# Layer 0's attention scores: from four-pass products of 48 rows to three one-pass products of exact 12-bit halves, 64 rows per head

## The chip, the cores and the metric

The kernel runs on one core of a Trainium2 chip. The metric is the device time of a whole execution in microseconds, from three runs; a profile is taken of a further execution. In the profile's names PE is TensorE (PEld its weight loads), DVE is VectorE, ACT is ScalarE, POOL is GpSimd, and SPq is the queue of DMA issues on SyncE.

## What is computed

Input x is 8 images of 384 channels and 32 x 32 pixels (1024 tokens), in fp32. Two layers follow. Layer 0 is attention over a group-normalized image, with a relative bias; layer 1 is a second attention (6 heads of 64, normalized q and k) and a feed-forward with binarized weights. The change is in layer 0:

```python
tokens = x.reshape(b, c, n).transpose(0, 2, 1)
qkv = (tokens @ qkv_w + qkv_b).reshape(b, n, 3, NUM_HEADS, HEAD_DIM)
...
q, k, v = (qkv[0], qkv[1], qkv[2])
scale = HEAD_DIM ** (-0.5)
attn = jnp.einsum('bhnd,bhmd->bhnm', q * scale, k)
attn = attn + _relative_bias(h, w, mlp_w1, mlp_b1, mlp_w2, mlp_b2)[None]
attn = jax.nn.softmax(attn, axis=-1)
out = jnp.einsum('bhnm,bhmd->bhnd', attn, v)
```

There are 8 heads of 48 dimensions; each head and image needs a score matrix of 1024 x 1024.

## The kernel before, in words

Layer 0 (`_layer0`) works image by image. For each image it projects q and k (`project_qk`, L464), then v (`project_v`, L498), and then runs 32 units. A unit (pair, h, m2) is one pair of heads (j = 0 and 1), one half h of the 1024 queries and 256 of the 1024 keys.

- `project_qk` makes, for three tiles of 128 rows and for q and k, a product of six fp32 matmul calls, three blocks of input channels times two halves of 512 tokens (L475); each call is two records in the profile. VectorE evicts q with bias and scale (L485), ScalarE evicts k with its bias (L489). A tile holds two heads of 48 rows in the lower parts of its two 64-row halves; the 16 rows left over in each half carry a third of the heads of pair 3, which six DMAs an image (L492) gather into pair 3's tile.
- `scores` (L522) issues for a unit eight fp32 matmuls (L529): 48 rows (the head's dimensions) by 64 keys, over 512 queries. j picks the upper or lower 64 rows of the array, c the left or right 64 columns, so that four of them have a quarter of the array each. Then it calls `weigh` for the unit two before, and after that VectorE adds the bias out of the table `grow` while it reads PSUM (L540), and ScalarE takes the exponential (L544).
- `weigh` (L549) multiplies a unit's exponentials with v, eight fp32 matmuls of 64 x 64 (L560), into one accumulator for a pair and half; after four units ScalarE and VectorE evict it (L568, L571), and after both halves `divide` (L574) writes the row sums to memory, reads them spread out (L588), has GpSimd take the reciprocal (L589), writes it (L590) and, some steps later, reads it back over 64 rows (L597) for a multiplication on GpSimd (L601).
- `project_out` for the image before comes at unit 3: 36 records of L624, three VectorE adds with the residual (L640), which was loaded by L634, and three writes of 512 KB (x<-res, L643).
- PSUM has four buffers of two banks (`mm2`). The accumulator holds one of them, a unit's two score tiles hold two. Exponentials, residuals and the pieces of the bias table share nine buffers of 512 KB (`etile`).

The order on each engine is the order of the calls: the pools and semaphores only add waits. Work that is spread over the units is hung on `_Later`, whose `step()` is called after each block of a projection and after each unit. In image 0 the relative bias is built this way: a table of 8 x 3969 values is written to memory (L387), and 32 pieces (head h, quarter c) are read from it, each by four DMAs on the SP queue (`grow_load`, L399, first into `etile` buffers named wide, later into oT) and turned by a copy (`grow_turn`, L409 on ScalarE for even c, L411 on VectorE for odd c). All these DMAs, and those of q and k, the residuals and the reciprocals, go through the one SP queue in order. A DMA there also waits until the eighth before it has landed.

The feed-forward of layer 1 already uses one-pass matmuls: L1578 and L1629 take operands of type F32R, an fp32 that was split into a rounded part and a remainder, and are one record for each call, with 128 x 128 weights.

Of the kernel before, what the change touches and what calls it, by code (L numbers as in the profile page):

```python
# [27 lines left out]
P = 128  # L28
QP = P // 2
# [12 lines left out]
FR = D0 // NF0  # L42
HID = 192
# [144 lines left out]
def _layer0(tc, ins, x1, sums, shared, weights, beside):  # L188
# [9 lines left out]
    with ExitStack() as ctx:  # L198
        const = ctx.enter_context(tc.tile_pool(name="a_const", bufs=1))
        qkp = ctx.enter_context(tc.tile_pool(name="a_qk", bufs=NP0))  # L200
        ep = ctx.enter_context(tc.tile_pool(name="a_e", bufs=9))
# [5 lines left out]
        def etile(name, shape=(P, N)):  # L207
            return ep.tile(list(shape), F32, tag="e", name=name)
# [44 lines left out]
        def load(b):  # L253
# [15 lines left out]
        assert FR == S0 - D0  # L269
        both = shared.weights("w0")  # L270
        wqk = both[:, 0 : KC * 2 * C].rearrange(
            "p (k s h d) -> p k s h d", k=KC, s=2, d=S0
        )
        wv = both[:, KC * 2 * C :].rearrange("p (k c) -> p k c", k=KC)
        bqk = const.tile([P, 2, NF0], F32, tag="bqk", name="bqk")
# [21 lines left out]
        def place_weights_qk():  # L297
            whole = 2 * NF0 * D0
            for s in range(2):
                nc.vector.tensor_copy(  # L300
                    wqk[:, :, s, :, 0:D0],
                    raw[:, :, s, 0:whole].rearrange("p k (h d) -> p k h d", d=D0),
                )
                for j in range(2):
                    at = whole + j * D0
                    nc.vector.tensor_copy(
                        wqk[:, :, s, j::2, D0:S0],
                        raw[:, :, s, at : at + D0].rearrange("p k (c d) -> p k c d", d=FR),
                    )

        def load_bias_qk():
            with nc.allow_non_contiguous_dma(reason="a bias, once"):
                for j in range(2):
                    for row, n, at, step in (
                        (j * S0, D0, j * D0, 2 * D0),
                        (j * S0 + D0, FR, (2 * NF0 + j) * D0, FR),
                    ):
                        for s in range(2):
                            nc.sync.dma_start(
                                bqk[row : row + n, s],  # L320
                                bass.AP(
                                    qkv_b.tensor, qkv_b.offset + s * C + at, [[1, n], [step, NF0]]
                                ),
                            )
# [139 lines left out]
        def project_qk(b, xn):  # L464

            qk = {
                pair: qkp.tile([P, 2, N], F32, tag="qk", name=f"qk{b}_{pair}") for pair in range(NP0)
            }
            for pair in range(NF0):
                t = qk[pair]  # L470
                for s in range(2):
                    pq = mm2(f"pq{b}_{pair}_{s}")
                    for k in range(KC):
                        for h in range(NH):
                            nc.tensor.matmul(  # L475
                                pq[:, h],
                                wqk[:, k, s, 2 * pair : 2 * pair + 2, :].rearrange(
                                    "p h d -> p (h d)"
                                ),
                                xn[:, k, ts(h, HALF)],  # L480
                                start=(k == 0), stop=(k == KC - 1),
                            )
                    bias = bqk[:, s, pair : pair + 1]
                    if s == 0:
                        nc.vector.tensor_scalar(  # L485
                            t[:, s], flat2(pq), bias, D0**-0.5, ALU.add, ALU.mult
                        )
                    else:
                        nc.scalar.activation(t[:, s], flat2(pq), AF.Identity, bias=bias)  # L489
                    later.step()  # L490
                for j in range(2):
                    nc.sync.dma_start(  # L492
                        qk[NF0][j * S0 + pair * FR : j * S0 + (pair + 1) * FR],
                        t[j * S0 + D0 : (j + 1) * S0],
                    )
            return qk
# [25 lines left out]
        def scores(b, qk, u, weigh):  # L522
            pair, h, m2 = u
            s = [mm2(f"s{b}_{pair}_{h}_{m2}_{j}") for j in range(2)]
            for i in range(2):
                for c in range(2):
                    for j in range(2):
                        rows = slice(j * S0, j * S0 + D0)
                        nc.tensor.matmul(  # L529
                            s[j][ts(c, QP), i], qk[pair][rows, 1, ts(4 * m2 + 2 * i + c, QP)],  # L530
                            qk[pair][rows, 0, ts(h, HALF)], start=True, stop=True,
                        )
# [155 lines left out]
        qk = project_qk(0, first)  # L688
        project_v(0, first)
        for b in range(B):  # L690
            held = []
            for i, u in enumerate(units):
# [8 lines left out]
                if i == 3 and b > 0:  # L701
                    project_out(b - 1, residuals(b - 1, etile), range(NF0))
                if b == B - 1:
                    for at, work in beside:
                        if at == i:
                            work()
                later.step()
            if b + 1 < B:
                qk = project_qk(b + 1, xn)
# [1197 lines left out]
```

## Time and profile before

| what | value |
|---|---|
| median of 3 runs | 3038.4 us (3035.8 to 3039.46) |
| span of the profiled execution, first to last instruction | 3031.8 us |
| median less that span | 6.6 us |
| mean granted TensorE clock | 0.999 |
| records on TensorE, busy | 18902, 3010.9 us |
| DMA traffic | 153.47 MB, mean 51 GB/s |
| layer 0's scores, L529 | 4096 records, 607.8 us busy |
| layer 0's weighing, L560 | 4096 records, 603.8 us busy |

The profile gives no time of its execution but the span, so sums are made against the span. "Busy" of a group is the time in which at least one of its instructions ran; since matmuls overlap, a group's mean duration is far longer than the distance from one start to the next. The timeline merges neighbours of one group into a line: start, time from the first start to the last end, and how many.

### The profile page before, as it was taken

What the parts mean: (1) busy time and instruction counts of PE and PEld (TensorE: products, weight loads), DVE (VectorE), ACT (ScalarE), POOL (GpSimd) and SP (SyncE); (2) the same over time, 40 slices, a digit from 0 to 9 for tenths busy, and PEclk for the clock granted to TensorE, in tenths of its full rate; (3) what the DMA queues carried; (4) which work ended last, traced back from release to release, by engine and by line L of the source; (5) the groups of instructions that cost most, each with busy time, mean ns of one, the idle gap of its engine ahead of it and who ended that gap; (6) DMA issues with size and microseconds to landing.
All of it is one profiled execution on the core that took longest, in us unless ns stands there. A gap on an engine that the chain in (4) does not pass through costs nothing.

```text
span 3031.8 us, 45645 instructions
## 1 busy us (share of the span) xinstructions
PE 3010.9 (99%) x18902; PEld 1622.9 (54%) x18902; DVE 1777.3 (59%) x1765; ACT 1401.8 (46%) x1757; POOL 470.2 (16%) x314
## 2 busy tenths in 40 slices
PE   8999999999999999999999999999999999999999
PEld 3555546455554645555545655655655655645453
DVE  3746637374654727364565765765765755755646
ACT  2633526253452615254463553553653543653534
POOL 2111102121110202102202202202202202211110
PEclk9999999999999999999999999999999999999999
DMA  7512020210202021121401101101101101102011
GB/s 199 146 26 83 19 83 17 72 37 19 83 19 83 23 72 30 26 99 51 116 27 37 50 16 37 50 23 30 50 23 30 50 23 30 50 16 72 16 51 38
DMA packets 102425, 153.47 MB, mean 51 GB/s; under 512 B 59648, under 2 KB 63216, under 8 KB 101184
## 3 DMA queue, kind: packets, MB, share of 16 engines
q1 hardware_dynamic: 98944, 148.63, 17.0%
q8 instruction: 152, 2.49, 0.3%
q10 hardware_dynamic: 3264, 1.82, 0.2%
q14 instruction: 65, 0.53, 0.1%
HBM read 112.29 MB, written 29.07 MB: 47 GB/s over the span
## 4 chain that ended last, share of the span: by engine, by line
PE 93%; DVE 2%; DMA 2%; SPq 1%; ACT 1%; POOL 0%; issue 0%; DVEq 0%; ACTq 0%; POOLq 0%
PE s L529 15%; PE o L560 15%; PE s L1337 11%; PE o L1386 11%; PE pq L475 8%; PE y2p L1629 6%; PE pq L1193 5%; PE pp L624 4%; PE pv L1274 4%; PE y1p L1578 4%; PE pp L1483 4%; PE pv L503 4%; SPq L399 1%; PE sum L1413 1%; PE hs L1222 1%; DVE lun L1530 1%
## 5 line engine op out<-in xcount | busy, mean ns | idle before, releaser
L544 ACT ACTIVATE e<-e 128x1024 f32<-128x1024 f32 x512 | 535.0, 1057 | 441.1 <-DVE e L540 419.9
L540 DVE TENSOR_TENSOR e<-s,grow 128x1024 f32<-128x1024 f32 x512 | 601.1, 1218 | 186.3 <-PE s L529 186.3
L529 PE MATMUL s<-qk 48*64 48x512 f32 x4096 | 607.8, 591 | 2.8 <-DVE e L540 2.7
L560 PE MATMUL o<-e,v 64*64 64x512 f32 x4096 | 603.8, 589 | 0.0
L1348 ACT ACTIVATE e<-s,kc 128x512 f32<-128x512 f32 x768 | 463.9, 694 | 170.6 <-PE s L1337 160.0
L1337 PE MATMUL s<-qk,qk 64*64 64x512 f32 x3072 | 418.3, 592 | 0.2
L1386 PE MATMUL o<-e,v 64*64 64x512 f32 x3072 | 414.8, 590 | 0.0
L529 PEld LDWEIGHTS s<-qk 48*64 48x64 f32 x4096 | 242.2, 132 | 222.1 <-issue 74.9
L560 PEld LDWEIGHTS o<-e,v 64*64 64x64 f32 x4096 | 266.7, 133 | 171.0 <-issue 63.0
L1363 DVE TENSOR_TENSOR t<-t,e 128x1024 f32<-128x1024 f32 x192 | 230.9, 1221 | 53.9 <-ACT e L1348 53.9
L1337 PEld LDWEIGHTS s<-qk,qk 64*64 64x64 f32 x3072 | 153.5, 132 | 189.9 <-issue 110.3
L1193 PE MATMUL pq<-bx,wqkv 128*128 128x512 f32 x576 | 254.1, 596 | 0.7 <-ACT tra L1165 0.7
L475 PE MATMUL pq<-xn,w 128*128 128x512 f32 x576 | 251.8, 598 | 0.0
L1386 PEld LDWEIGHTS o<-e,v 64*64 64x64 f32 x3072 | 157.6, 133 | 171.1 <-issue 143.8
L589 POOL TENSOR_TENSOR inv<-sums,over 128x16 f32<-128x16 f32 x32 | 92.8, 2900 | 956.9 <-DMA sums<-sd 785.4
L475 PEld LDWEIGHTS pq<-xn,w 128*128 128x128 f32 x576 | 109.4, 191 | 142.4 <-issue 139.9
L1193 PEld LDWEIGHTS pq<-bx,wqkv 128*128 128x128 f32 x576 | 107.8, 190 | 143.5 <-issue 139.7
L1360 DVE TENSOR_TENSOR t<-e,e 128x1024 f32<-128x1024 f32 x96 | 114.1, 1224 | 83.0 <-ACT e L1348 83.0
L1565 DVE TENSOR_REDUCE parts<-y 128x1 f32<-128x1024 f32 x75 | 90.1, 1217 | 93.7 <-ACT y L1562 93.2
L1243 POOL TENSOR_TENSOR hc<-hc,rsqrt 128x32 f32<-128x32 f32 x24 | 139.0, 5793 | 2.0
L1209 ACT ACTIVATE qsq<-pq 128x1024 f32<-128x1024 f32 x48 | 49.2, 1025 | 190.1 <-DVE qk L1203 101.9
L485 DVE TENSOR_SCALAR qk<-pq,bqk 128x1024 f32<-128x1024 f32 x24 | 30.8, 1283 | 178.3 <-PE pq L475 178.3
(166 smaller groups left out, 3034.3 us busy)
## 6 DMA issues: line engine op xcount, KB each, us to landing
rb<-rd SPq DMA_DIRECT2D x110, 256.0 KB
xn<-in_x_dram SPq DMA_DIRECT2D x24, 512.0 KB
res<-in_x_dram SPq DMA_DIRECT2D x24, 512.0 KB
x<-res SPq DMA_DIRECT2D x24, 512.0 KB
bx<-x SPq DMA_DIRECT2D x8, 1536.0 KB
rq<-hi SPq DMA_DIRECT2D x48, 256.0 KB
out_dram<-bx SPq DMA_DIRECT2D x23, 512.0 KB
wide<-table SPq DMA_DIRECT2D x80, 114.2 KB
```

The lines of the kernel that those rows point to most:

```text
L475: nc.tensor.matmul(pq[:, h], wqk[:, k, s, 2 * pair : 2 * pair + 2, :].rearrange("p h d -> p (h d)"), xn[:, k, ts(h, HALF)], start=(k == 0) ...
L529: nc.tensor.matmul(s[j][ts(c, QP), i], qk[pair][rows, 1, ts(4 * m2 + 2 * i + c, QP)], qk[pair][rows, 0, ts(h, HALF)], start=True, stop=True,)
L540: nc.vector.tensor_add(e.rearrange("p (i q) -> p i q", i=2), s[j], bass.AP(near.tensor, near.offset, [near.ap[0], [-QROWS * IW, 2], [1, HA ...
L544: nc.scalar.activation(e, e, AF.Exp)
L560: nc.tensor.matmul(po[ts(j, S0), r], v[keys, 2 * m2 + i, 2 * pair + j, :], es[j][keys, ts(i, HALF)], start=(m2 == 0 and i == 0), stop=(m2 ...
L1193: nc.tensor.matmul(pq[:, h], wqkv[:, k, s * C + pair * P : s * C + (pair + 1) * P], xt[:, k, ts(h, HALF)], start=(k == 0), stop=(k == KC - 1),
L1243: nc.gpsimd.tensor_tensor(c, c, rsqrt.to_broadcast(list(c.shape)), ALU.pow)
L1337: nc.tensor.matmul(s[j][ts(c, QP), i], qk[pair, 1][rows, ts(4 * m2 + 2 * i + c, QP)], qk[pair, 0][rows, ts(h, HALF)], start=True, stop=True,)
L1348: nc.scalar.activation(e[:, ts(i, HALF)], s[j][:, i], AF.Exp, scale=kc[:, pair, j, m : m + 1])
L1363: nc.vector.tensor_add(total[j], total[j], e)
L1386: nc.tensor.matmul(po[ts(j, D1), r], v[keys, 2 * m2 + i, at : at + D1], es[j][keys, ts(i, HALF)], start=(m2 == 0 and i == 0), stop=(m2 == ...
L1629: nc.tensor.matmul(py[m][:, h], w2[:, k, ts(m, P)], supply.parts[k][i][:, ts(h, HALF)], start=(k == 0 and i == 0), stop=(k == FC - 1 and i ...
```

## The change

q and k are split, on eviction, into a rounded part (high) and what is left (low), both of type F32R, so that a product of parts needs one pass of TensorE. q . k is then the sum of four products of parts. To fill 64 rows of the array, the head's 48 dimensions are cut into 32 (DA) and 16 (DB):

- The first 32 dimensions of a head give 64 rows of alternating high and low. `q1` and `k1` in the same order give high.high + low.low; `k1x`, with the two swapped, gives the cross products.
- The last 16 dimensions give 32 rows, twice: `q2` holds them twice, `k2` once in order and once swapped, so one product gives all four.

So a head's scores are three accumulated products of 64 rows, and each matmul takes 128 keys at once: 12 matmul calls a unit of one record each, instead of 8 of two. The two heads of a pair still have the upper and the lower 64 rows.

The columns of the weights are put in the order that this needs (two blocks of 128 with the first 32 dimensions of four heads each, one block with the last 16 of all eight), and q's scale goes into weights and bias. The six evictions of an image each become one on ScalarE (high) and one on VectorE (low). Both parts are written to memory (12 writes of 512 KB an image), and the tiles q1, k1, k1x, q2 and k2 of a pair are read back in their layout by nine DMAs (2.5 MB a pair), `load_pair`: for pair 0 inside the projection, for pair p + 1 in the second unit of pair p. All of them are issued on the SP queue; the six DMAs of L492 go. The projection's `etile` buffers hold the parts until they are written, and there are eight of them instead of nine.

```diff
@@ -40,6 +40,9 @@
+DA = 32
+DB = D0 - DA
+NB0 = C // P
...
-        qkp = ctx.enter_context(tc.tile_pool(name="a_qk", bufs=NP0))
-        ep = ctx.enter_context(tc.tile_pool(name="a_e", bufs=9))
+        qkp = ctx.enter_context(tc.tile_pool(name="a_qk", bufs=2))
+        ep = ctx.enter_context(tc.tile_pool(name="a_e", bufs=8))
...
-        def etile(name, shape=(P, N)):
-            return ep.tile(list(shape), F32, tag="e", name=name)
+        def etile(name, shape=(P, N), dtype=F32):
+            return ep.tile(list(shape), dtype, tag="e", name=name)
...
         def place_weights_qk():
-            whole = 2 * NF0 * D0
             for s in range(2):
-                nc.vector.tensor_copy(
-                    wqk[:, :, s, :, 0:D0],
-                    raw[:, :, s, 0:whole].rearrange("p k (h d) -> p k h d", d=D0),
-                )
-                for j in range(2):
-                    at = whole + j * D0
-                    nc.vector.tensor_copy(
-                        wqk[:, :, s, j::2, D0:S0],
-                        raw[:, :, s, at : at + D0].rearrange("p k (c d) -> p k c d", d=FR),
-                    )
+                given = raw[:, :, s].rearrange("p k (h d) -> p k h d", d=D0)
+                for at, n, d0, d in ((0, H0 * DA, 0, DA), (H0 * DA, H0 * DB, DA, DB)):
+                    to = wqk[:, :, s, at : at + n].rearrange("p k (h d) -> p k h d", d=d)
+                    of = given[:, :, :, d0 : d0 + d]
+                    if s == 0:
+                        nc.vector.tensor_scalar_mul(to, of, D0**-0.5)
+                    else:
+                        nc.vector.tensor_copy(to, of)
...
+            nc.gpsimd.tensor_scalar(bqk[:, 0], bqk[:, 0], D0**-0.5, 1.0, ALU.mult, ALU.mult)
...
         def project_qk(b, xn):
-            qk = {
-                pair: qkp.tile([P, 2, N], F32, tag="qk", name=f"qk{b}_{pair}") for pair in range(NP0)
-            }
-            for pair in range(NF0):
-                t = qk[pair]
-                for s in range(2):
-                    pq = mm2(f"pq{b}_{pair}_{s}")
-                    for k in range(KC):
-                        for h in range(NH):
-                            nc.tensor.matmul(
-                                pq[:, h],
-                                wqk[:, k, s, 2 * pair : 2 * pair + 2, :].rearrange(
-                                    "p h d -> p (h d)"
+            halves, qk = {}, {}
+            blocks = [(blk, s) for blk in (NB0 - 1, *range(NB0 - 1)) for s in range(2)]
+            for n, (blk, s) in enumerate(blocks):
+                pq = mm2(f"pq{b}_{blk}_{s}")
+                for k in range(KC):
+                    for h in range(NH):
+                        nc.tensor.matmul(
+                            pq[:, h], wqk[:, k, s, ts(blk, P)], xn[:, k, ts(h, HALF)],
+                            start=(k == 0), stop=(k == KC - 1),
+                        )
+                bias = bqk[:, s, blk : blk + 1]
+                high = etile(f"hq{b}_{blk}_{s}", dtype=F32R)
+                low = etile(f"lq{b}_{blk}_{s}", dtype=F32R)
+                nc.scalar.activation(high, flat2(pq), AF.Identity, bias=bias)
+                nc.vector.scalar_tensor_tensor(
+                    low, flat2(pq), bias, high.bitcast(F32), ALU.add, ALU.subtract
+                )
+                there = dram.tile([P, 2, N], F32, tag=f"hl{blk}{s}", name=f"hl{b}_{blk}_{s}")
+                for x, part in enumerate((high, low)):
+                    nc.sync.dma_start(there[:, x], part.bitcast(F32))
+                halves[blk, s] = there
+                if n in (2, 3, 4):
+                    load_pair(b, 0, halves, qk, n - 2)
+                later.step()
+            return halves, qk
+        def load_pair(b, pair, halves, qk, part):
+            blk, row = pair // 2, pair % 2 * S0
+            if part == 0:
+                at = 2 * pair * DB
+                for name, s in (("q2", 0), ("k2", 1)):
+                    t = qkp.tile([P, N], F32R, tag=name, name=f"{name}_{b}_{pair}")
+                    src = halves[NB0 - 1, s]
+                    qk[pair, name] = t
+                    for j in range(2):
+                        first = src.offset + (at + j * DB) * 2 * N
+                        if s == 0:
+                            nc.sync.dma_start(
+                                t[ts(j, S0)].bitcast(F32),
+                                bass.AP(src.tensor, first, [[0, 2], [N, 2 * DB], [1, N]]),
+                            )
+                            continue
+                        for y in range(2):
+                            nc.sync.dma_start(
+                                t[j * S0 + y * DA : j * S0 + (y + 1) * DA].bitcast(F32),
+                                bass.AP(
+                                    src.tensor, first + y * N,
+                                    [[2 * N, DB], [N - 2 * y * N, 2], [1, N]],
                                 ),
-                                xn[:, k, ts(h, HALF)],
-                                start=(k == 0), stop=(k == KC - 1),
                             )
-                    bias = bqk[:, s, pair : pair + 1]
-                    if s == 0:
-                        nc.vector.tensor_scalar(
-                            t[:, s], flat2(pq), bias, D0**-0.5, ALU.add, ALU.mult
-                        )
-                    else:
-                        nc.scalar.activation(t[:, s], flat2(pq), AF.Identity, bias=bias)
-                    later.step()
-                for j in range(2):
-                    nc.sync.dma_start(
-                        qk[NF0][j * S0 + pair * FR : j * S0 + (pair + 1) * FR],
-                        t[j * S0 + D0 : (j + 1) * S0],
-                    )
-            return qk
+                return
+            for name, s, y in (("q1", 0, 0),) if part == 1 else (("k1", 1, 0), ("k1x", 1, 1)):
+                t = qkp.tile([P, N], F32R, tag=name, name=f"{name}_{b}_{pair}")
+                src = halves[blk, s]
+                qk[pair, name] = t
+                nc.sync.dma_start(
+                    t.bitcast(F32),
+                    bass.AP(
+                        src.tensor, src.offset + row * 2 * N + y * N,
+                        [[2 * N, S0], [N - 2 * y * N, 2], [1, N]],
+                    ),
+                )
...
         def scores(b, qk, u, weigh):
             pair, h, m2 = u
             s = [mm2(f"s{b}_{pair}_{h}_{m2}_{j}") for j in range(2)]
+            terms = (("q1", "k1"), ("q1", "k1x"), ("q2", "k2"))
             for i in range(2):
-                for c in range(2):
+                for n, (q, k) in enumerate(terms):
                     for j in range(2):
-                        rows = slice(j * S0, j * S0 + D0)
                         nc.tensor.matmul(
-                            s[j][ts(c, QP), i], qk[pair][rows, 1, ts(4 * m2 + 2 * i + c, QP)],
-                            qk[pair][rows, 0, ts(h, HALF)], start=True, stop=True,
+                            s[j][:, i], qk[pair, k][ts(j, S0), ts(2 * m2 + i, P)],
+                            qk[pair, q][ts(j, S0), ts(h, HALF)],
+                            start=(n == 0), stop=(n == len(terms) - 1),
                         )
             finish = weigh()
...
-        qk = project_qk(0, first)
+        halves, qk = project_qk(0, first)
...
+                if u[1:] == (0, 1) and u[0] + 1 < NP0:
+                    for part in range(3):
+                        load_pair(b, u[0] + 1, halves, qk, part)
...
-                qk = project_qk(b + 1, xn)
+                halves, qk = project_qk(b + 1, xn)
```

The bias of q and k is loaded by ten DMAs instead of eight, in the new order of rows.

## The prediction

> **What bounds the kernel now.** I read the page first (busy shares, chain, costliest groups), then the timeline of TensorE through the score loop and over every change of tile shape, then the startup on VectorE, ScalarE and the SP queue, then busy time by stretch.
>
> ```profile
> span 3031.8 us, 45645 instructions
> PE 3010.9 (99%) x18902; PEld 1622.9 (54%) x18902; DVE 1777.3 (59%) x1765; ACT 1401.8 (46%) x1757; POOL 470.2 (16%) x314
> PE 93%; DVE 2%; DMA 2%; SPq 1%; ACT 1%; POOL 0%; issue 0%; DVEq 0%; ACTq 0%; POOLq 0%
> L540 DVE TENSOR_TENSOR e<-s,grow 128x1024 f32<-128x1024 f32 x512 | 601.1, 1218 | 186.3 <-PE s L529 186.3
> L529 PE MATMUL s<-qk 48*64 48x512 f32 x4096 | 607.8, 591 | 2.8 <-DVE e L540 2.7
> L560 PE MATMUL o<-e,v 64*64 64x512 f32 x4096 | 603.8, 589 | 0.0
> ```
>
> TensorE is the bound nearly everywhere: 93% of the chain, and it almost never waits ahead of L529 or L560. Each matmul of fp32 is two records (4096 for 2048 calls). A unit (pair, half, m2) has 16 records of scores, then 16 of weighing. The mean of 591 ns is latency, not cost; the timeline gives the cost:
>
> ```profile
> 87.51 2.01 PE L529 MATMUL s<-qk 48*64 48x512 f32 x16
> 89.23 2.01 PE L560 MATMUL o<-e,v 64*64 64x512 f32 x16
> 90.95 2.01 PE L529 MATMUL s<-qk 48*64 48x512 f32 x16
> ```
>
> From start to start 1.72 us for 16 records, 3.44 us a unit: four tiles of 64x64 run side by side, four "quads" of 429 ns. Now the changes of tile shape, which the score loop of before has none of (48x64 and 64x64 are one shape):
>
> ```profile
> 220.76 0.59 PE L475 MATMUL pq<-xn,w 128*128 128x512 f32 x1
> 221.29 0.66 PE L560 MATMUL o<-e,v 64*64 64x512 f32 x4
> ...
> 223.91 1.04 PE L560 MATMUL o<-e,v 64*64 64x512 f32 x8
> 224.88 1.24 PE L503 MATMUL pv<-w,xn 128*128 128x384 f32 x3
> ```
>
> L475 has a pitch of 0.43, yet L560 starts 0.53 after it. Two quads take 1.04 (0.43 + 0.59 + the stagger); the first two after this change take 1.09 in the same view (0.05 more). Back: the last quad starts at 223.91 + 0.43 = 224.34, L503 0.54 later, and its three records take 1.24 where a pitch of 0.32 gives 1.13. So a change costs about 0.09 at once, and then one more weight load that nothing hides: 0.05 for 64 columns, 0.10 for 128. All changes that I looked at, between shapes of 128, 64 and 32 columns, cost this within 0.01 (the load in proportion to the columns). One-pass matmuls stand in the feed-forward:
>
> ```profile
> 1685.10 0.73 PE L1629 MATMUL y2p<-hy,w 128*128 128x512 f32 x2
> 1685.67 0.62 PE L1629 MATMUL y2p<-ly,w 128*128 128x512 f32 x2
> ...
> 1715.41 0.62 PE L1629 MATMUL y2p<-ly,w 128*128 128x512 f32 x2
> 1715.96 1.52 PE L1337 MATMUL s<-qk,qk 64*64 64x512 f32 x12
> ```
>
> A pair takes 0.62 = 0.39 + 0.23: pitch 0.232. The first pair after a change (1685.10) takes 0.73, the load again; from a one-pass matmul (1715.41 + 0.23 = 1715.64) into 64x64 it is 0.32, 0.09 over the pitch.
>
> **What the Trainium skill says.** "TensorEngine Tiling (Array Packing)", Key Properties: a change of tiling mode, not merely of tile, drains the array; the trace agrees, at 0.09 us each. The same page, Available Configurations, lists 64x128 as two independent tiles; no row here shows that shape at work. "TensorE: Matmul & The Clock Gate", LDWEIGHTS: a load takes columns / 1.2 ns, whatever the rows, which is 53 and 107 ns for 64 and 128; the trace agrees (0.05 and 0.10 left open after a change). The same page, Back-to-back issue gap, gives 216 ns for 512 columns; two such passes make the 429 of fp32, but the one-pass matmuls, a new load before each, stand at 232, and I take the trace.
>
> **The change, part by part.**
>
> *Scores, at the steady unit.* Before 4 x 429 = 1716 ns. After: 12 records in six pairs (j = 0 and 1 side by side), each 128 columns wide: 6 x 232 = 1392. Saved 324. But scores are now 64x128 and weighing stays 64x64, so each unit changes shape twice: into scores 0.09 + 0.10, into weighing 0.09 + 0.05, together 0.33. Unit after: 1392 + 1716 + 330 = 3438 against 3432. Some 30 units an image, 8 images: 240 x 6 ns = +1.5 us. The pair's pitch isn't shown: 216 (the page's) gives 240 x 6 x 16 ns = -23 us, 240 gives +12. I take 232, since each pair again loads 128 fresh columns.
>
> *The first three score groups of an image* have no weighing between them. TensorE would be 1 us quicker, but the third needs the banks that the second add of unit 0 frees: two adds of L540 take 2.35 us a unit, so weighing starts some 5.6 us after the first score, as before (240.56 to 246.19). Nothing.
>
> *VectorE and ScalarE in the unit:* unchanged, 2 x 1.2 and 2 x 1.06 of 3.44 us. A bank is freed about 1.3 us after the scores end and is wanted 1.8 after (weighing and the changes); hidden.
>
> *Projection:* as many matmuls (36 an image). Each of six evictions becomes a ScalarE one (1.11, L489) and then a VectorE one (1.24, as L1618): 2.4 us in 5.15 us of matmuls, with three PSUM buffers. Hidden. The rows of e that it borrows come back after a write of about 2.6 us (x<-res of 512 KB, issue to landing), two blocks (10 us) before their next use. Hidden.
>
> *Transfers of images 1 to 7.* Twelve writes of 512 KB, and 2.5 MB of loads for each pair. In the projection the queue is nearly empty:
>
> ```profile
> 190.20:221.20 31.00, 31.00 (x75) 13.58 (x72) 4.58 (x4) 4.04 (x4) 0.00 (x0) 1.00 0.10 17
> 248.00:256.00 8.00, 8.00 (x49) 3.51 (x42) 3.79 (x4) 4.55 (x5) 0.00 (x0) 1.00 0.89 347
> 36.50:80.00 43.50, 43.50 (x140) 21.11 (x138) 16.03 (x24) 8.70 (x12) 12.81 (x9) 1.00 0.90 226
> ```
>
> (The last two columns are DMA share and GB/s.) 8.5 MB in 31 us is 275 GB/s, where 347 are moved at 0.89. The last load of pair 0 is issued after the fifth block's eviction, about 29 us in, and lands by 34; its scores come 50 us in (31 + 3.6 + 15.7 of projecting v). Pairs 2 and 3 are loaded from units 9 and 17, behind a reciprocal row that waits 6 us for GpSimd on the same queue; nine issues at about 0.5 and the landing make 14 us, wanted after 24. Residual loads come 6 us later than now, and so do VectorE's adds on them, with two PSUM buffers still free in time. All hidden; if the cover of a pair's load were gone, it would cost its excess over 24 us.
>
> *Transfers of image 0: not hidden.* The bias table is spread over 80 loads through the same SP queue, back to back, and VectorE waits for them at the first scores:
>
> ```profile
> 37.11 5.41 SPq L399 DMA_DIRECT2D wide<-table  x12
> 42.62 1.25 SPq L492 DMA_DIRECT2D qk<-qk  x2
> ...
> 83.28 0.65 DVE L411 COPY grow<-wide 128x480 f32<-128x480 f32 x1 [0.89 <-DMA wide<-table]
> ...
> 126.52 0.59 ACT L409 COPY grow<-oT 128x480 f32<-128x480 f32 x1 [2.52 <-DMA oT<-table]
> ...
> 131.59 1.51 PE L529 MATMUL s<-qk 48*64 48x512 f32 x11 [1.81 <-DVE e L540]
> ```
>
> In the built order of the changed kernel the second block's writes stand ahead of the first of these loads: its matmuls end as the first k block's do now, at 38.85; ScalarE 1.1, VectorE 1.3, issue 0.4 give 41.7, against 37.11: +4.6. Then eight more writes and nine loads stand among them in place of six copies, 11 issues more at 0.49 (43 us for 86): +5.4. Together +10. By bytes: 4.2 + 2.6 - 0.8 = 6 MB more at 390 GB/s is 15 us, and the stretch has 0.10 x 43.5 = 4 to spare: +11. I take +11, since unit 1 already waits for its copy (83.28). Bounds: 5, if half is absorbed, to 17. Later in image 0 nine loads stand between the reciprocal row and the table load for which ScalarE already waits 2.52 us (126.52, after which TensorE lost time, 131.59): 9 x 0.48 = +4.3; bounds 0 and 6.
>
> *Setup* (weights placed by four copies for six, two more bias loads, a small GpSimd multiply): some 1 us in queues that wait for the statistics; nothing.
>
> *Sum:* 1.5 + 11 + 4.3 = +17 on a span of 3031.8, so 3049. The runs' median, 3038.4, lies 6.6 above that span; adding this, 3055.
>
> **The rivals.** (a) *A change between two 64-row shapes costs less than the trace's changes.* No row shows 64x128 to 64x64. If it were free, 240 x 0.33 = 79 us come off: 2976. It is faster than before once two changes cost under 0.33 - 17/240 = 0.26 us. Against it: 128x128 to 128x32, which changes columns alone, also pays 0.09. A pitch of 216 would give 3032. Together 0.15. (b) *The table loads are absorbed* (the 0.90 share is waiting, not work): about 3041, 0.10. (c) *A transfer comes late in every image*, say a pair's load by 5 us: 7 x 5 to 10 more, 3090 to 3125. For: one SP queue with waits for GpSimd in it; against: the slacks above. 0.12. (d) *The two row tiles don't run side by side, so it isn't 64 rows per head in one pass time:* 240 x 6 x 232 ns = +334, 3390. Against: quads run four abreast now. 0.08.
>
> **How the numbers follow.** Forecast 0.55 (3045 to 3075); the rest as given. A measurement of this kernel can tell 0.2%, 6 us. Faster 0.15, within 0.10, slower 0.75. The range leaves out (d) and about half of (a) and the late third of (c): 3027 to 3100.
>
> **What would show it.** The score loop's period from weighing to weighing near 3.44 us; score pairs 0.23 apart; 0.32 from the last score pair to weighing and 0.52 back; the first exponentials some 11 us later; the copy near 130 us waiting about 7; no wait of TensorE for loads after image 0. A period of 3.1 or 4.8 us would prove me wrong, and so would TensorE waiting at a pair's first score.

## The result, and the profile after

The changed kernel takes 3449.2 us (median of 4 runs, 3448.3 to 3451.0); the kernel before, run beside it, takes 3037.1 (3035.3 to 3039.5). The ratio is 1.136, with a 95% interval of 1.134 to 1.137. Slower was forecast, but at 3055, with a range that ended at 3100.

These are the lines of the changed kernel's page that answer to those of before (span, TensorE, the chain that ended last, the scores):

```profile
span 3446.6 us, 44133 instructions
PE 3095.0 (90%) x17878; PEld 1558.5 (45%) x17878; DVE 1804.9 (52%) x1787; ACT 1428.2 (41%) x1781; POOL 469.3 (14%) x315
PE 50%; DMA 10%; DVE 2%; POOL 1%; SPq 1%; issue 1%; ACT 1%; DVEq 0%; POOLq 0%; ACTq 0%
L569 PE MATMUL s<-q,k 64*128 64x512 f32 x2048 | 434.8, 442 | 281.1 <-DMA k<-hl 145.0
```

The chain of the changed kernel could be followed back only to 1215 us, so its shares add up to 66% of the span; in that part alone DMA has 10% of the span, where it had 2% in the whole chain of before. Ahead of the scores (L569) TensorE now stands idle for 281.1 us, over half of it for `k<-hl`, the reload of k; it was 2.8 before. That is the first thing which the forecast had excluded.

The score loop itself is what was forecast. In the timeline of TensorE (start, time to the last end, instructions merged, idle time before and its releaser), first an undisturbed unit, then the four long waits of image 1; the line of VectorE (DVE) belongs to the second of them:

```profile
162.75 0.40 PE L569 MATMUL s<-q,k 64*128 64x512 f32 x2
163.08 1.95 PE L601 MATMUL o<-e,v 64*64 64x512 f32 x16
164.95 0.51 PE L569 MATMUL s<-q,k 64*128 64x512 f32 x2
...
339.41 5.80 PE L665 MATMUL pp<-oT,wp 128*128 128x512 f32 x7 [4.54 <-DMA oT<-oT]
...
368.76 3.80 DVE L681 SCALAR_TENSOR_TENSOR res<-pp,bp,res 128x1024 f32<-128x1024 f32 x3 [33.38 <-DMA res<-in_x_dram]
370.10 0.79 PE L569 MATMUL s<-q,k 64*128 64x512 f32 x1 [12.45 <-DVE res L681]
...
423.77 0.79 PE L569 MATMUL s<-q,k 64*128 64x512 f32 x2 [8.51 <-DMA k<-hl]
...
465.35 0.79 PE L569 MATMUL s<-q,k 64*128 64x512 f32 x2 [10.54 <-DMA k<-hl]
```

The next weighing starts at 166.56, so a unit is 3.48 us (3.44 forecast); pairs of scores stand 0.235 apart in the same view (162.06 to 162.53 is two), and the last pair is 0.33 ahead of weighing (0.32 forecast). Then the waits: 4.54 us for the gather of oT (six DMAs, L652, that bring pair 3's result into the rows that the output projection reads), 12.45 for the residual adds, 8.51 and 10.54 for k at the first score of pairs 2 and 3. A table of the stages, each from the first projection matmul of an image to that of the next, shows how regular this is:

| kernel | image 0 | images 1 to 6, each | from image 7 to the end |
|---|---|---|---|
| before | 166.1 | 174.5 | 1794.9 |
| changed | 250.0 | 222.0 | 1841.5 |

So 84 us are lost in image 0, and 47 in each of the seven others (the last is in the last column). Image 1 by windows, and two short windows in it (the columns are the busy time of each engine, the granted clock, the DMA share and GB/s):

```profile
273.40:496.00 222.60, 184.72 (x1056) 84.16 (x1052) 99.99 (x97) 77.42 (x79) 25.84 (x15) 0.90 0.36 109
...
451.00:455.00 4.00, 3.81 (x32) 1.56 (x28) 2.89 (x3) 2.73 (x3) 0.00 (x0) 1.00 0.14 49
457.00:461.00 4.00, 0.00 (x0) 0.00 (x0) 0.00 (x0) 0.00 (x0) 0.00 (x0) 0.52 0.13 45
```

TensorE is idle for 37.9 of the 222.6 us, 36 of them in these four waits. The rest of the loss is clock: after each wait the granted clock is about half for a few us, and in this image it is 0.90 on average.

The two short windows point to the cause. In them, while TensorE uses up its last work and then waits, the DMA share is 0.13 to 0.14 of 16 engines, which is as much as two engines, and 45 to 49 GB/s (between and after them other loads run, at a share of up to 0.95). In the SP queue of the changed kernel the loads of pair 3 stand so:

```profile
442.14 1.12 SPq L512 DMA_DIRECT2D q<-hl  x2
...
453.68 0.58 SPq L530 DMA_DIRECT2D k1x<-hl  x1
```

A DMA has landed when its semaphore has risen by 16. By the increments in the trace, the two loads of L512 (256 KB each, tile q2) land 11.5 and 17.1 us after their issue; each rises once about 1 us after issue and then only twice more, late, so 14 of the 16 come at once and two engines carry it. The other seven land between 460.5 and 466.5, all behind them, and show the same two engines: of the 16 increments of the k load issued at 443.30, fourteen come 2.2 to 3.1 us after issue and the last two after 15.6 and 17.2. The issue of k1x at 453.68 had itself waited for the first q2 load, the eighth DMA before it. Loads of twice the size (xn, L259), issued on this queue in the same image, had landed in 3.9 to 6.4.

**Theory.** L512's source is `[[0, 2], [N, 32], [1, N]]`: the same 32 rows twice, with a dimension of 2 outermost. The Trainium skill, "DMA: Bandwidth & Descriptors", in the section on why a DMA increments its semaphore by 16, says that the slowest dimension larger than 1 of both sides sets the number of engines, the largest number up to 16 that divides both, and that engines which take no part post their increments at once. This agrees with the 14 early increments. So 512 KB a pair go over two engines, with the eighth part of every load that uses all sixteen, and whatever is queued behind waits for these two. **Rivals:** the 128 MB of added traffic as such; the added issues on the SP queue; row tiles or tile changes that cost more than steady stretches show.

### The profile page after: what moved, and what is told of

Same layout as the page of the kernel before. It is cut to its first block, busy times and chain, and to the rows that moved or that the text cites. A ratio compares the mean times of both kernels' runs of the same rounds, so it can differ in the third digit from the quotient of the medians.

```text
span 3446.6 us, 44133 instructions
## 1 busy us (share of the span) xinstructions
PE 3095.0 (90%) x17878; PEld 1558.5 (45%) x17878; DVE 1804.9 (52%) x1787; ACT 1428.2 (41%) x1781; POOL 469.3 (14%) x315
## 2 busy tenths in 40 slices
DMA packets 138917, 281.32 MB, mean 82 GB/s; under 512 B 64144, under 2 KB 67712, under 8 KB 138448
## 3 DMA queue, kind: packets, MB, share of 16 engines
q8 instruction: 144, 2.36, 0.3%
## 4 chain that ended last, share of the span: by engine, by line
PE 50%; DMA 10%; DVE 2%; POOL 1%; SPq 1%; issue 1%; ACT 1%; DVEq 0%; POOLq 0%; ACTq 0%
PE s L1381 10%; PE o L1430 9%; PE y2p L1673 5%; PE pq L1237 5%; PE pv L1318 4%; PE y1p L1622 4%; DMA q<-hl 4%; PE pp L1527 4%; PE o L601 3%; PE s L569 3%; DMA k1x<-hl 2%; PE pq L477 1%; DMA hl<-lq 1%; PE sum L1457 1%; PE pp L665 1%
## 5 line engine op out<-in xcount | busy, mean ns | idle before, releaser
L569 PE MATMUL s<-q,k 64*128 64x512 f32 x2048 | 434.8, 442 | 281.1 <-DMA k<-hl 145.0
L601 PE MATMUL o<-e,v 64*64 64x512 f32 x4096 | 521.3, 627 | 0.0
L569 PEld LDWEIGHTS s<-q,k 64*128 64x128 f32 x2048 | 222.5, 198 | 529.8 <-issue 181.0
L1430 PE MATMUL o<-e,v 64*64 64x512 f32 x3072 | 414.9, 590 | 0.0
L601 PEld LDWEIGHTS o<-e,v 64*64 64x64 f32 x4096 | 138.5, 139 | 259.9 <-issue 257.9
L569 PE MATMUL s<-q,k1x 64*128 64x512 f32 x1024 | 235.8, 423 | 6.2 <-DMA k1x<-hl 6.2
L1430 PEld LDWEIGHTS o<-e,v 64*64 64x64 f32 x3072 | 157.9, 133 | 170.8 <-issue 143.5
L485 DVE SCALAR_TENSOR_TENSOR lq<-pq,bqk,hq 128x1024 fp32r<-128x1024 f32 x48 | 61.6, 1283 | 255.9 <-ACT hq L484 212.6
L665 PE MATMUL pp<-oT,wp 128*128 128x512 f32 x288 | 139.4, 647 | 31.1 <-DMA oT<-oT 31.1
L484 ACT ACTIVATE hq<-pq,bqk 128x1024 fp32r<-128x1024 f32 x48 | 53.5, 1114 | 240.6 <-PE pq L477 156.5
```

Of the source, the lines that this page charges most:

```text
L569: nc.tensor.matmul(s[j][:, i], qk[pair, k][ts(j, S0), ts(2 * m2 + i, P)], qk[pair, q][ts(j, S0), ts(h, HALF)], start=(n == 0), stop=(n == ...
L601: nc.tensor.matmul(po[ts(j, S0), r], v[keys, 2 * m2 + i, 2 * pair + j, :], es[j][keys, ts(i, HALF)], start=(m2 == 0 and i == 0), stop=(m2 ...
L665: nc.tensor.matmul(pps[b, m][:, h], (wp[:, k] if k < NF0 else wl)[:, ts(m, P)], oT[:, k, ts(h, HALF)], start=(k == 0), stop=(k == (NF0 if ...
L1430: nc.tensor.matmul(po[ts(j, D1), r], v[keys, 2 * m2 + i, at : at + D1], es[j][keys, ts(i, HALF)], start=(m2 == 0 and i == 0), stop=(m2 == ...
```

## The experiments

The stages of all runs, in us, as in the table above:

| run | image 0 | images 1 to 6, each | image 7 to the end | median | ratio to before (95%) |
|---|---|---|---|---|---|
| changed | 250.0 | 222.0 | 1841.5 | 3449.2 | 1.134 to 1.137 |
| e1 q2 interleaved | 207.1 | 175.5 | 1800.1 | 3081.2 | 1.0125 to 1.0159 |
| e2 before, two engines | 193.0 | 174.7 | 1796.5 | 3062.6 | 1.0062 to 1.0096 |
| e3 before, sixteen engines | 173.8 | 174.5 | 1796.8 | 3042.5 | 1.0006 to 1.0020 |
| e4 q2 on ScalarE's queue | 247.9 | 205.2 | 1824.2 | 3327.7 | 1.0926 to 1.0977 |
| e5 before, image 0's traffic | 207.5 | 174.5 | 1795.9 | 3075.4 | 1.0112 to 1.0146 |
| e6 four engines | 229.1 | 195.8 | 1813.0 | 3240.2 | 1.0647 to 1.0682 |
| e7 e1, table later | 214.4 | 175.0 | 1800.6 | 3088.4 | 1.0154 to 1.0188 |
| e8 e1, two units | 208.9 | 174.3 | 1795.1 | 3076.0 | 1.0119 to 1.0153 |
| e9 q2 last | 241.0 | 215.7 | 1838.3 | 3399.3 | 1.1178 to 1.1216 |
| e10 ahead of reciprocals | 233.3 | 202.9 | 1814.3 | 3293.3 | 1.0840 to 1.0881 |

### e1: the same loads over sixteen engines

```diff
-    bass.AP(src.tensor, first, [[0, 2], [N, 2 * DB], [1, N]]),
+    bass.AP(src.tensor, first, [[N, 2 * DB], [0, 2], [1, N]]),
...
-    t[j * S0 + y * DA : j * S0 + (y + 1) * DA].bitcast(F32),
+    t[j * S0 + y : (j + 1) * S0 : 2].bitcast(F32),
```

> The changed kernel, with one thing different: the two copies of q's last rows in tile q2 lie row by row (row 2r and 2r + 1 the same), so the load's source has 32 rows outermost and not 2; k2 is laid out to match. Same bytes, same number of DMAs, same arithmetic. Theory (a load whose outermost dimension is 2 goes over 2 of the 16 DMA engines, takes over 12 us, and everything behind it on the SP queue waits for these two): the q2 loads land in under 6 us and the time falls to 3055 to 3080 (my 3055, and 240 units of 3.475 us as the changed kernel's trace shows them in place of 3.438, +9). Rival 1 (the 128 MB of traffic that the change adds, or HBM): within 20 us of 3449. Rival 2 (nine more issues and waits on the SP queue for each pair): within 20 us of 3449. Rival 3 (row tiles or tile shapes on TensorE cost more than the steady stretches show): within 50 us of 3449.

Measured: 3081.2 us, 1 us over the theory's range and far from every rival's. The page of this kernel:

```profile
span 3083.4 us, 44133 instructions
PE 3021.6 (98%) x17878; PEld 1530.7 (50%) x17878; DVE 1808.0 (59%) x1787; ACT 1429.1 (46%) x1781; POOL 470.0 (15%) x315
PE 87%; DMA 3%; DVE 3%; SPq 1%; issue 1%; ACT 1%; POOL 0%; DVEq 0%; ACTq 0%; POOLq 0%
```

The instructions and bytes are the same (44133, 281.32 MB; k2's rows move to match, in loads that have 16 increments in both kernels), and 363 of 415 us of span are gone. In image 1 the q2 loads of pairs 2 and 3 land in 3.5 to 4.1 us, with 16 increments one by one (pair 1's, behind the loads of xn, in 6.4 and 7.0, over the 6 of the theory). Image 1, the stretch of the table loads in image 0, and the stretch in which pair 3's nine loads run:

```profile
230.40:404.90 174.50, 173.87 (x1057) 79.88 (x1053) 100.33 (x97) 77.54 (x79) 25.85 (x15) 1.00 0.44 139
40.40:102.00 61.60, 45.15 (x120) 23.16 (x118) 19.58 (x27) 9.61 (x13) 12.80 (x9) 0.83 0.97 275
...
365.00:376.00 11.00, 11.00 (x92) 4.91 (x95) 8.36 (x8) 6.63 (x8) 0.00 (x0) 1.00 0.95 276
```

Set the first line beside image 1 of the changed kernel: 222.6 less 174.5 is 48.1 us, 37.3 of them idle time of TensorE (37.9 less 0.6) and 10.8 busy time at the lower clock. The last line is what 0.14 and 49 GB/s were: 0.95 and 276 GB/s. This run kept the traffic, the issues and the tiles of the three rivals, so all three fall for images 1 to 7. Image 0 keeps a loss of 41 us, against 15 forecast; e5 and e7 are for that. (Over the kernel before that ran beside it the median is up by 42 us, the span by 52 over the profiled one. A run's time is 1.8 us above its span; the profile of before is of an execution some 5 us faster than its median, that of e1 of the slowest of its four, 4 us above its median. Differences of a few us in image 0 or in the last column of the table are therefore not sure.)

### e2 and e3: the two-engine loads put into the kernel before

```diff
+        spare = const.tile([P, N], F32, tag="spare", name="spare")
...
+    if u[1:] == (0, 1):
+        for j in range(2):
+            nc.sync.dma_start(
+                spare[ts(j, S0)],
+                bass.AP(x.tensor, x.offset + (b * C + 32 * j) * N, [[0, 2], [N, 32], [1, N]]),
+            )
```

They stand in the second unit of all four pairs; the change issues those of pair 0 inside the projection. In e3 each is two loads of `[[N, 32], [1, N]]` into 32 rows.

> The kernel before, and for each pair two more loads of 256 KB with an outermost dimension of 2, issued where the change issues its own, into a tile that nobody reads (the output is that of before). Theory (queueing behind two engines, not only late data of q and k): slower by 100 to 350 us, with reciprocals, residuals and statistics landing late. Rival (only q and k tiles that TensorE itself waits for cost time): within 20 us of 3037. If traffic alone counts, as slow as the same bytes spread over 16 engines.

> The kernel before, and for each pair the same bytes as in the run with an outermost dimension of 2, in four loads of 128 KB with 32 rows outermost, into a tile that nobody reads. Theory: within 15 us of 3037, since each load is spread over all engines and gone in a few us. Rival (traffic or SP issues as such): as slow as the run with an outermost dimension of 2.

Measured: 3062.6 and 3042.5 us. My theory missed e2: an image grows by 0.2 us, not by 12 or more, and the median by 23 us over the kernel before that ran beside it; the rival's range is missed as well, by 6 us. The loads behave as in the changed kernel (two of 256 KB landed after 10.9 and 15.2 us, and the reciprocal's loads behind them after 15.2), but in the kernel before nothing that TensorE needs soon stands behind them. Only image 0, where the table loads do, pays 27 us. So a load on two engines is not slow work that adds up; two of them are a delay of 13 to 20 us for themselves and what follows on their engines, and cost what that exceeds the slack. e3, the same bytes on all engines, stays within its 15 us: its median is 3 us above that of before, and the table shows 8 us in image 0 and none in images 1 to 6.

### e4: q2 from another queue

```diff
-    nc.sync.dma_start(
+    nc.scalar.dma_start(
         t[ts(j, S0)].bitcast(F32),
```

> The changed kernel with only the two q2 loads of a pair issued by ScalarE in place of SyncE; they keep their outermost dimension of 2. If what costs is that SP's own queue fills up behind them (eight in flight), over half of the loss goes: 3150 to 3250. If it is the two engines themselves, which the loads of both queues share, and q2's own late landing: 3300 to 3449. If the loads have nothing to do with it: 3449 within 20.

Measured: 3327.7 us, within the second case. An image is 205 us, 17 of the 47 lost come back. That is about what the SP queue's standing still was worth. The rest is the two engines, which both queues share: behind q2, issued by ScalarE, SP's own writes of 512 KB landed after 9.7 and 10.8 us, where those before them took 2.6 to 3.3, and again the last two increments alone were late. The Trainium skill says so too, in "DMA: Bandwidth & Descriptors" under "Issuing engines are not separate DMA queues": DMAs run on the same 16 engines and interleave there, whoever starts them.

### e6: four engines

```diff
-    nc.sync.dma_start(
-        t[ts(j, S0)].bitcast(F32),
-        bass.AP(src.tensor, first, [[0, 2], [N, 2 * DB], [1, N]]),
-    )
+    for y in range(2):
+        nc.sync.dma_start(
+            t[j * S0 + y * DA : j * S0 + (y + 1) * DA].bitcast(F32),
+            bass.AP(src.tensor, first, [[N, 4], [4 * N, DB // 2], [1, N]]),
+        )
```

> The changed kernel with q2 in four loads of 128 KB whose outermost dimension is 4 in place of two of 256 KB with 2 (the rows come in another order than k2's, so the scores are not those of the reference). Theory: 512 KB a pair go over 4 engines, which is half of the 18 us that two engines took; with the loads behind it 12 to 16 us, close to the 16 us between issue and use in the changed kernel. An image takes 174 to 182 us, the time is 3080 to 3140. If the outermost dimension does not set the number of engines: 3081 within 10. If the run over 16 engines was fast for another reason than the number of engines: over 3300.

Measured: 3240.2 us, 196 us an image, between 222 (two) and 175 (sixteen): the number of engines sets the loss, but more of it was left than the 174 to 182 us that I had forecast. In the trace 12 increments come at once, so there are four engines; pair 1's q2 loads land in 7.9 to 11.2 us, and the last of the pair's loads (eleven here) 19.0 us after the first issue (313.6 to 332.6 in image 1). I had set the slack at 16 us; the next runs show that it is less.

### e9 and e10: order and start of the nine loads

e9 issues q2 last of the nine: `load_pair` makes q2 in a fourth part, after k1 and k1x. e10 issues the nine before the second unit's code; this is its edit:

```diff
+    if u[1:] == (0, 1) and u[0] + 1 < NP0:
+        for part in range(3):
+            load_pair(b, u[0] + 1, halves, qk, part)
     done = held.pop(0) if len(held) == LAG else None
...
-    if u[1:] == (0, 1) and u[0] + 1 < NP0:
-        for part in range(3):
-            load_pair(b, u[0] + 1, halves, qk, part)
```

> The changed kernel with the two q2 loads of each pair issued last of the nine in place of first; they keep their outermost dimension of 2. Theory (the 18 us that these two take on their two engines, of which the other loads' parts on these engines are no more than 5): the other seven now land in under 10 us, q2 still some 23 us after the first issue, and TensorE waits at a pair's third product in place of its first: an image takes 205 to 222 us, the time 3330 to 3449. Rival (it is mostly the other seven, queued behind q2, that come late): an image under 190 us, the time under 3200.

> The changed kernel, two-engine q2 loads and all, with the nine loads of a pair issued ahead of the second unit's code and so ahead of the reciprocal row of the pair before on the SP queue, in place of behind it. Theory: in the changed kernel the nine are issued 12.7 us ahead of a pair's first score (442.1 and 454.8 in image 1) and take 24.3 until the last lands, so TensorE waits some 10; issued ahead of the row they have 20 to 26 us, and the waits for pairs 2 and 3 fall from 8.5 and 10.5 to under 3 each. The residuals behind pair 1's loads (12.5 us) and the gather (4.5) stay. An image takes 198 to 208 us in place of 222, the time is 3270 to 3350. Rival (the two engines are a bound for all traffic, so waits only move elsewhere): within 40 us of 3449.

Measured: 3399.3 and 3293.3 us, 216 and 203 us an image, both within their theory's ranges. In e9 the seven others land in 2.3 to 7.8 us, pair 3's q2 loads 16.2 and 21.2 us after the first of the nine. TensorE does the first two products of pairs 2 and 3 and then waits twice, 1.75 + 4.53 and 2.75 + 4.29 us in image 1, where it was 8.51 and 10.54. For pair 3:

```profile
442.41 0.39 PE L571 MATMUL s<-q,k1x 64*128 64x512 f32 x2
445.55 0.79 PE L571 MATMUL s<-q,k 64*128 64x512 f32 x1 [2.75 <-DMA q<-hl]
450.64 1.19 PE L571 MATMUL s<-q,k 64*128 64x512 f32 x3 [4.29 <-DMA rb<-rd]
```

Each of these waits ends within 0.15 us of the landing of a q2 load (407.32 and 412.30, 445.51 and 450.50), so q2 itself is late, and not only what is behind it. (The view puts the last wait down to `rb<-rd`.) The residuals behind pair 1's q2 still cost 10.24. In e10 the wait for pair 2 is gone and pair 3's is 2.36 us, with residuals (12.78) and gather (4.22) as in the changed kernel. The forecast of e10 rested on the slack: the changed kernel issues pair 3's loads at 442.14 and is ready for them at 454.8, which is 12.7 us, and they take 24.3. The difference, 11.6, is the 10.5 us wait within about 1 us (k1, which is wanted before k1x, landed at 465.2).

### e5 and e7: image 0

e5 adds to the kernel before what the change moves in image 0, as writes from a tile at rest (`move(P, P)` is two of 512 KB):

```diff
+        def move(*rows):
+            for n in rows:
+                there = dram.tile([n, N], F32, tag=f"move{n}", name=f"move{len(moved)}")
+                moved.append(there)
+                nc.sync.dma_start(there, spare[0:n])
...
+    if b == 0:
+        move(P, P)
+        n = 2 * pair + s
+        if n in (2, 3, 4):
+            move(*((64, 64, 32, 32, 32, 32), (P,), (P, P))[n - 2])
...
+    if b == 0 and u[1:] == (0, 1) and u[0] + 1 < NP0:
+        move(64, 64, 32, 32, 32, 32, P, P, P)
```

> The kernel before, and in image 0 alone as many bytes as the change moves there by the places where it moves them (12 times 512 KB in the projection, 2.5 MB for each of the four pairs, 16.8 MB in all), all as writes to memory from a tile that never changes, so that nothing waits for them. Theory (image 0 is bound by the DMA engines, which the table loads already fill, so bytes are simply added): the period from the first projection of image 0 to that of image 1 grows from 166 by 30 to 50 us, and the time to 3065 to 3090. Rival (it is the waits of the SP queue for the evictions, and TensorE waiting for q and k): under 15 us.

Measured: 3075.4 us, image 0 at 207.5, which is 41.4 more, where e1 has 41.0. The table loads and what is added to them fill the engines; the window of e5 that answers to e1's 40.40:102.00:

```profile
37.00:100.00 63.00, 47.87 (x121) 21.38 (x119) 15.41 (x23) 7.89 (x11) 12.79 (x9) 0.84 0.96 279
```

Share 0.96 and 279 GB/s, against 0.97 and 275 in e1. No engine's work in e5 needs the added writes, so e1's loss in image 0 is the added transfers and not waits for q and k. e5 adds the issues along with the bytes and does not part the two; that the engines are busy to 0.96 speaks for the bytes.

e7 is e1 with 12 pieces of the table loaded during the projections in place of 20, and the others one a unit:

```diff
-    for i, n in enumerate((3, 3, 3, 3, 2, 2, 2, 2)):
+    for i, n in enumerate((2, 2, 2, 2, 1, 1, 1, 1)):
...
-        for i in range(len(parts) - 20):
...
+        for i in range(len(parts) - 12):
```

> The changed kernel with q2 interleaved over 16 engines (3081), and in image 0 only 12 of the 32 pieces of the bias table loaded during the projections in place of 20; the other 20 follow one a unit. Theory (image 0 waits for DMA engines that serve pieces before their time): the first exponentials, at 101 us now, come at 80 to 92 us, and the time falls by 10 to 30 us, to 3050 to 3070. Rival (image 0's total of bytes sets its end whatever the order): within 8 us of 3081.

Measured: 3088.4 us, 7 more than e1 and not 10 to 30 less (11 more when each is set against the kernel before that ran beside it). The first add before the exponentials comes at 87.0 us in place of 101.0, but then TensorE waits 13.59 us up to 155.1, since VectorE waits (13.94) for a piece that lies behind pair 2's nine loads on the queue, and 14.89 from 186 on. The theory fell, and the rival's number held for the medians, if barely: serving the pieces later gains nothing, and this order only moved the waits.

### e8: what a change of tile shape costs

e8 is e1 with the scores of two units ahead of the weighing of two. The heart of the loop:

```diff
+    s = [scores(b, qk, u0, 0), scores(b, qk, u0, 1)]
+    es0 = [exponentials(b, u0, 0, s[0])]
+    s.append(scores(b, qk, u1, 0))
+    es0.append(exponentials(b, u0, 1, s[1]))
+    s.append(scores(b, qk, u1, 1))
+    finishes = [weigh(b, *done) for done in held]
+    es1 = [exponentials(b, u1, i, s[2 + i]) for i in range(2)]
```

> The changed kernel with q2 interleaved over 16 engines (3081), and the scores of two units issued together ahead of the weighing of two units, with a score tile for 128 keys of both heads in place of one head's 256 keys. So TensorE changes its tile shape once for two units where it changed for each. Forecast's term (two changes cost 0.33 us a unit): about 240 x 0.165 = 40 us less, two units in 6.6 us where they take 6.95, time 3035 to 3055. Rival (a change costs nothing, the 0.33 are waits for VectorE or score banks): within 10 us of 3081, or slower, since the fourth score tile now waits for the first add.

Measured: 3076.0 us, inside the rival's 10. The timeline of TensorE in e8, where nothing else interferes:

```profile
331.00 0.50 PE L568 MATMUL s<-q,k 64*128 64x512 f32 x2
...
337.54 0.50 PE L568 MATMUL s<-q,k 64*128 64x512 f32 x2
```

Two units take 6.54 us and not 6.95: two changes cost 0.41 (0.33 forecast), so the rival has the time right and the reason wrong. It is given back elsewhere: the next two units take 6.79, since the fourth score tile waits for VectorE's first add of this pair of units, which ends at 339.78, and the units around the output projection wait some 0.8 to 1 us each. An image gains 1 us net. The time is not clearly below e1's (1.0136 of the kernel before, against 1.0142, with intervals that overlap), and still 1.4% behind the kernel before.

## Why the prediction was wrong, step by step

- **Scores at the steady unit: right.** 3.475 in place of 3.438 us: pairs 0.235 and not 0.232 apart, the two changes 0.35 to 0.41 and not 0.33. Over 240 units 9 us more than forecast. Rivals (a) and (d) fall with this: a change between two shapes of 64 rows costs what the other changes do, and two row tiles do run side by side.
- **First three score groups, VectorE and ScalarE, evictions, setup: right.** In image 2 of e1 the first score to the first weighing is 5.68 us (5.63 before) and the projection 31.1 (31.1 before); image 0's projection starts at 23.3 (24.1 before).
- **"Transfers of images 1 to 7 ... All hidden": the step that failed.** I counted bytes and issues and took every load as spread over all engines, which L512's pattern forbids; the view to use was the access pattern itself. It cost 47 us an image and 43 in image 0 (changed less e1). The forecast's 14 us, from the reciprocal row's first issue to the landing of the last load, are 31.1 in the changed kernel (435.4 to 466.5 in image 1), for a score that is ready after 19.4. Two of its terms were also too kind, and only e1's sixteen engines hid that. In place of the 14 us e1 has 18.1 (357.8 to 375.9). I had them wanted after 24 us; pair 3's first score in e1 is at 377.15, after 19.3. So on sixteen engines the slack was 1.2 us and not 10. The residuals, "6 us later, still in time", were behind pair 1's q2 loads, and VectorE waited 33.4 us for them in image 1. (The 8.5 MB and 275 GB/s of the projection count 512 KB as 0.5 MB; it is 8.9 MB and 287 GB/s, which changes nothing here.)
- **Image 0: the mechanism was right, its size was not.** Forecast 15.3, measured 41 in e1. I took 6 MB for the first part, at 390 GB/s less 4 us of spare time, and the start of 4.6 us as contained in it. The 390 is the rate of another stretch (347 at a share of 0.89); the table's own (226 at 0.90) is 251 with all engines busy, which makes 24 us of 6 MB. Measured, the table loads start 3.3 us later and take 61.4 us in place of 42.3 from the first issue to the last, and the first exponentials come 20.9 us later (102.2 in e1, 81.3 before). For the second part I counted issue slots (4.3 us), though the engines are nearly as full there (share 0.92 from 102 to 140 us in e1): from the first table load to 165 us e1 moves 31.45 MB at 252 GB/s, where before it was 19.77 MB up to 130. The 11.7 MB more at that rate are 46 us, and e5 shows that the transfers alone give 41. Rival (b) falls.
- **Rival (c), a transfer late in every image,** was the right kind in the right place ("a pair's load"), at 12% and 5 to 10 us an image. The price was a guess about the queue's order, where the engines would have given it, at 24 GB/s each by the prediction's own 390 for sixteen: q2's 524 KB and an eighth of the other 2.1 MB are 786 KB, 16 us at 49 GB/s for two, beside what is issued before and after.
- **What would show it** was well chosen: the period held, the wait at a pair's first score was named as the proof against me, and it was there 10 us long.

Not settled: how much of the 10.8 us of slower clock in image 1 belongs to which wait, how much of image 0's loss is issues and not bytes, and whether a lower number of bytes in image 0 could be had without changing the table.

## What to carry to other kernels

Read the outermost dimension of every new DMA before its bytes: a repeat of two placed outermost leaves fourteen engines without a part of it, and putting the repeat inside cost nothing here and gave back 363 us of the span. Then ask what stands behind that DMA in its queue and on its engines, and compare its landing with the time at which the next consumer is ready, both taken from the trace (12.7 against 24.3 us here); the same load cost 0.2 us an image where nothing urgent was behind it. Where the DMA share is already 0.9, price added bytes at the rate of that stretch and not of another (251 and not 390 GB/s here), with no spare time.

## What the runs showed of the hardware that I had not expected

- Two engines moved 45 to 49 GB/s, four gave landings of 7.9 to 11.2 us for pair 1's q2, sixteen moved 276 GB/s. In a window of few us in which nothing else runs, the DMA share shows the number of engines (0.13 to 0.14, two of sixteen); the increments show it for each load (3 separate ones for two engines, 5 for four, 16 for sixteen).
- Waits of 8 to 12 us on TensorE cost more than their length: the granted clock was 0.50 for the 4.7 us after the wait that ended at 465.3, and image 1 lost 10.8 us of busy time at a lower clock beside 37 of idle time.
- Two loads of q2 took 17.7 us from the first issue to the second landing, and loads of the same queue with only an eighth of their bytes on these engines landed 16 to 19 us after issue, though fourteen of their sixteen parts were there long before: a part of a load that is late makes the whole load late.
